# The first image's tokens are loaded and normalized among the turning of the weights

## Chip, cores and metric

The kernel runs on one core of a Trainium2 chip, as one program and one launch. The metric is the device time of that core in microseconds (us). A change of one part in five hundred, some 26 us, is about the smallest that a measurement of this kernel can tell from none.

A core has a matrix engine (TensorE, PE in the views), an engine for element-wise work and reductions (VectorE, DVE), one for functions of single elements (ScalarE, ACT), a general one (GpSimd, POOL), and a fifth that only issues transfers (SyncE, SP). Each takes its instructions in the order in which the program gives them. Transfers between the chip's memory (HBM) and the cores' memory (SBUF) are issued from the queues of SP, ACT and POOL. PE writes its results to a small memory divided into banks (PSUM).

## Reference

The input is `x`, four images of 64 x 64 tokens with 128 channels. Two layers follow each other; only the first part of the first layer bears on the change.

```python
# layer 0: group normalization, then a selective scan in three orders of the tokens
x = x + L0(_gn(x))
# layer 1: attention with 16 heads of 8 and a small network, then 64 experts of which tokens are picked
t = t + L1_attn(_ln_t(t)); t = t + L1_ffn(_ln_t(t))

def _gn(v, G=32, eps=1e-5):          # per image: mean and variance over 4 channels x 4096 tokens
    g = v.reshape(B_, H_, W_, G, C_ // G)
    m = jnp.mean(g, axis=(1, 2, 4), keepdims=True)
    s = jnp.var(g, axis=(1, 2, 4), keepdims=True)
    return ((g - m) / jnp.sqrt(s + eps)).reshape(v.shape)

xz = in_proj_w @ x                   # 128 channels to 2 x 256: x and z
u = silu(causal_conv1d(x, conv_w) + conv_b)              # 4 taps along the tokens
dt, B, C = split(x_proj_w @ u); delta = softplus(dt_w @ dt + dt_b)
h = h * exp(delta * A) + delta * u * B; y = sum(h * C)   # 16 states for each of 256 channels
y = (y + D * u) * silu(z)
```

The scan runs over the tokens forward, backward, and in an order that steps through 16 slices, each with weights of its own. `out_proj_w` brings the sum of the three back to 128 channels.

## The kernel before

The whole program is unrolled. Its work falls into stages.

**The weights.** `scan_weights` (L135) brings in `in_proj_w` and `out_proj_w` and turns them: PE transposes blocks of 128 x 128 into PSUM and DVE copies them out, to `w_z` and `w_out`. Then it does the same for each of the three orders ("directions"): `x_proj_w` (L155 to L163: 2 transposes, 12 small copies), `dt_proj_w` (L164 to L173: four transfers, two of them from SP's queue and two from ACT's), the biases and `D` (L174 to L180, seven transfers from ACT's queue with the taps) and the convolution, whose taps are folded into `in_proj_w`: for each of four taps DVE scales two blocks (L189), PE transposes them (L190) and DVE copies both out (L191). The raw weights lie in a pool `w_load`, closed at the end of the stage, with two slots of PSUM of its own.

**The inputs.** The class `Inputs` opens its pools after that (`i_const`, `i_big`, `i_piece`, `i_small`, and three slots of PSUM of two banks each), so that they may lie where the weights' pools lay. Its `norm(b)` (L270) brings in an image's tokens in four tiles `x_g` of 1024 tokens (512 KB each, L282, two slots), transposes each with eight transposes (L286), copies it to `xn` on ACT (L288), and takes statistics on DVE (L292). Two small matmuls sum them over groups of four channels (L297, L305), POOL raises the variance to the power -1/2 (L44, L45), and DVE scales the four pieces of `xn` (L313). `of_chunk` makes what the scan needs, for one direction and 1024 tokens: the convolution by PE (L378, 32 matmuls), silu on ACT (L385), the projection (L392, L395), `dt` (L414), softplus on ACT and PE (L418 to L436), the last addition on DVE (L441), and the product of delta and u (L446) for the first chunks. The results go to HBM from POOL's queue. The part from L414 to L441 is done for one chunk at a time (the flag `middle`), and each bank of PSUM that L436 fills comes free when L441 has read it. `gate` makes the silu of z.

**The scan of image 0.** `Scans.of_image` takes 384 steps of 128 rows (16 channels with 8 states) by 1024 tokens. A step is a scan on DVE (L538), the next step's product with B (L529) and the product with C (L543); ACT makes the exponentials (L522), PE sums over the states (L570). `decays` (L202), which comes first in this chain, waits until image 0 is normalized and then issues 96 small transfers of `A_log` from SP (L212).

**The order.** The code of the weights' stage is ordered by the framework's scheduler, which may also let an instruction of a later stage go ahead of it. Inside `tc.manual_schedule()` the program's own order holds on each engine. There, generators give their work in pieces that end with `yield`, and `Pace` runs them against each other. For all four images' inputs and the first image's scan it is this loop:

```python
            first = Pace(decays(nc, dirs, ws, inputs), scans.of_image(0, inputs.made, True))
            others = Pace(flow(inputs.pieces(range(nb)), 2, 10))
            while not first.done:
                others.run(1.5)
                first.run(1.0)
```

So `others` takes three pieces in every two rounds, one in a round and two in the next, and the scan one in each: the transfers and the exponential of a step in a round, its work on DVE in the next. `flow` keeps two of the inputs' generators going; the second starts when the one before has given ten pieces.

**The rest.** After that come image 0's opening, the attention of images 0 to 2 with the scans of images 1 to 3 beside it, image 3's attention, and the experts.

Of the kernel before, what the change touches and what calls it, by code (L numbers as in the profile page):

```python
# [11 lines left out]
F32 = mybir.dt.float32  # L12
# [4 lines left out]
P = 128  # L17
C = 128
L = 4096
NT = L // P  # L20
DI = 256
# [4 lines left out]
NC = L // T  # L26
NS2 = NS // 2
NB = DI // 8
# [103 lines left out]
        self.free += 1  # L132


def scan_weights(nc, const, load, load_ps, ident, in_proj_w, out_proj_w, dirs):  # L135

    w_z = const["fill"].tile([P, DI], F32, name="w_z")
    w_out = const["all"].tile([P, 2, C], F32, name="w_out")
    w_in = load.tile([P, 4, C], F32, tag="w_in", name="raw_in")
    nc.sync.dma_start(out=w_in, in_=in_proj_w.rearrange("(k p) c -> p k c", p=P))  # L140
    ps = load_ps.tile([P, 512], F32, tag="ps", name="ps_in")
    for m in range(2):
        nc.tensor.transpose(ps[:, m * P : (m + 1) * P], w_in[:, 2 + m, :], ident)
    nc.vector.tensor_copy(w_z, ps[:, :DI])
    raw = load.tile([P, DI], F32, tag="raw", name="raw_out")
    nc.sync.dma_start(out=raw, in_=out_proj_w)
    ps = load_ps.tile([P, 512], F32, tag="ps", name="ps_out")
    for m in range(2):
        nc.tensor.transpose(ps[:, m * P : (m + 1) * P], raw[:, m * P : (m + 1) * P], ident)
    nc.vector.tensor_copy(w_out.rearrange("p m c -> p (m c)"), ps[:, :DI])  # L150
    ws = []
    for i, d in enumerate(dirs):
        w = {}
        raw = load.tile([R + 2 * NS, DI], F32, tag="raw", name=f"raw_x{i}")
        nc.sync.dma_start(out=raw, in_=d["x_proj_w"])  # L155
        w["x"] = const["fill"].tile([P, 2, X_ROWS], F32, name=f"w_x{i}")
        nc.gpsimd.memset(w["x"], 0.0)
        for m in range(2):
            ps = load_ps.tile([P, 512], F32, tag="ps", name=f"ps_x{i}_{m}")
            k = R + 2 * NS  # L160
            nc.tensor.transpose(ps[:, :k], raw[:, m * P : (m + 1) * P], ident[:k, :k])
            for row, at, n in [(32 * g, 0, R) for g in range(4)] + [(B_ROW, R, NS), (C_ROW, R + NS, NS)]:
                nc.vector.tensor_copy(w["x"][:, m, row : row + n], ps[:, at : at + n])  # L163
        raw = load.tile([P, 2, X_ROWS], F32, tag="raw_dt", name=f"raw_dt{i}")  # L164
        nc.gpsimd.memset(raw, 0.0)
        for g in range(4):
            by = (nc.sync, nc.scalar)[g % 2]
            by.dma_start(out=raw[:, :, 32 * g : 32 * g + R], in_=d["dt_proj_w"].rearrange("(m p) r -> p m r", p=P))
        w["dt"] = const["fill"].tile([X_ROWS, 2, P], F32, name=f"w_dt{i}")
        ps = load_ps.tile([P, 512], F32, tag="ps", name=f"ps_dt{i}")  # L170
        for m in range(2):
            nc.tensor.transpose(ps[:X_ROWS, m * P : (m + 1) * P], raw[:, m, :], ident)
        nc.vector.tensor_copy(w["dt"].rearrange("r m p -> r (m p)"), ps[:X_ROWS, :DI])  # L173
        for name in ("conv_b", "dt_proj_b"):  # L174
            w[name] = const["fill"].tile([P, 2], F32, name=f"{name}{i}")
            nc.scalar.dma_start(out=w[name], in_=d[name].rearrange("(m p) -> p m", p=P))

        w["D"] = const["all"].tile([P, DI // 32], F32, name=f"D{i}")
        for g in range(4):
            nc.scalar.dma_start(out=w["D"][32 * g : 32 * g + 32], in_=d["D"].rearrange("(k p) -> p k", p=32))  # L180

        taps = load.tile([P, 2, 4], F32, tag="taps", name=f"taps{i}")
        nc.scalar.dma_start(out=taps, in_=d["conv_w"].rearrange("(m p) k -> p m k", p=P))
        w["conv"] = const["fill"].tile([P, 4, DI], F32, name=f"conv{i}")
        for k in range(4):
            ps = load_ps.tile([P, 512], F32, tag="ps", name=f"ps_cv{i}_{k}")
            for m in range(2):
                cut = load.tile([P, C], F32, tag="cut", name=f"cut{i}_{k}_{m}")
                nc.vector.tensor_scalar_mul(cut, w_in[:, m, :], taps[:, m, k : k + 1])  # L189
                nc.tensor.transpose(ps[:, m * P : (m + 1) * P], cut, ident)  # L190
            nc.vector.tensor_copy(w["conv"][:, k, :], ps[:, :DI])  # L191
        ws.append(w)
    for i, w in enumerate(ws):
        w["A"] = const["all"].tile([P, 2, NB // 2], F32, name=f"A{i}")
    return w_z, w_out, ws


def early(b, order, c):
# [17 lines left out]
class Inputs:  # L216
# [1 line left out]


    def __init__(self, tc, ctx, x, w_z, ws, cols, dram, ident):  # L220
        nc = self.nc = tc.nc
        self.x, self.w_z, self.ws, self.cols, self.dram, self.ident = x, w_z, ws, cols, dram, ident
        const = ctx.enter_context(tc.tile_pool(name="i_const", bufs=1))
        self.big = ctx.enter_context(tc.tile_pool(name="i_big", bufs=1))
        self.piece = ctx.enter_context(tc.tile_pool(name="i_piece", bufs=1))
        self.small = ctx.enter_context(tc.tile_pool(name="i_small", bufs=2))
        self.ps = ctx.enter_context(tc.tile_pool(name="i_ps", bufs=3, space=PSUM))

        group = const.tile([P, 32, 4], F32, name="group")
        nc.gpsimd.memset(group, 0.25)  # L230
        nc.gpsimd.affine_select(
            out=group, in_=group, compare_op=ALU.is_ge, fill=0.0,
            base=0, pattern=[[-4, 32], [0, 4]], channel_multiplier=1,
        )
        nc.gpsimd.affine_select(
            out=group, in_=group, compare_op=ALU.is_ge, fill=0.0,
            base=3, pattern=[[4, 32], [0, 4]], channel_multiplier=-1,
        )
        self.group = group.rearrange("p g r -> p (g r)")
        self.minus = const.tile([P, P], F32, name="minus")  # L240
        nc.vector.tensor_scalar_mul(self.minus, ident, -1.0)
        self.minus_one = column(nc, const, -1.0, "minus_one")
        self.made, self.sz, self.normed, self.sliced, self.gated = {}, {}, {}, {}, {}
        self.held, self.middle = 0, False

    def bank(self, name):
        while self.held == 3:
            yield WAIT
        self.held += 1
        return self.ps.tile([P, T], F32, tag="a", name=name)  # L250
# [4 lines left out]
    def pieces(self, images):  # L255

        for b in images:
            self.sz[b] = self.dram.tile([DI, L], F32, name=f"d_sz_{b}")
            yield self.norm(b)
            for order in range(3):  # L260
                if order == 2:
                    yield self.slices(b)
                for c in range(NC):
                    yield self.of_chunk(b, order, c)
                    third, at = divmod(order * NC + c, 3)
                    if at == 2:
                        yield self.gate(b, third)

    def norm(self, b):

        nc = self.nc
        while b - 1 in self.gated and self.gated[b - 1] < NC:
# [5 lines left out]
        nc.gpsimd.memset(xn[:, L + 3 :], 0.0)  # L278
        stats = self.small.tile([P, L // 512, 6], F32, tag="stats", name=f"stats_{b}")
        for g in range(NC):  # L280
            x_g = self.piece.tile([P, 8, C], F32, tag="x_g", bufs=2, name=f"x_{b}_{g}")
            nc.sync.dma_start(out=x_g, in_=xin[:, g * 8 : g * 8 + 8, :])  # L282
            yield
            ps = yield from self.bank(f"xt_{b}_{g}")
            for k in range(8):
                nc.tensor.transpose(ps[:, k * P : (k + 1) * P], x_g[:, k, :], self.ident)  # L286
            cut = xn[:, 3 + g * T : 3 + (g + 1) * T]
            nc.scalar.copy(cut, ps)  # L288
            self.leave()
            yield  # L290
            for k in range(2):
                nc.vector.bn_stats(stats[:, 2 * g + k, :], cut[:, k * 512 : (k + 1) * 512])  # L292
# [1111 lines left out]
def tile_kernel(tc, ctx, x, in_proj_w, dirs, out_proj_w, attn, gate, weight1, weight2, out):  # L1404


    nc = tc.nc
    nb = x.shape[0]
    ctx.enter_context(nc.allow_non_contiguous_dma(reason="small weight columns"))
    dram = ctx.enter_context(tc.tile_pool(name="dram", bufs=1, space=bass.MemoryType.DRAM))  # L1410
# [8 lines left out]
    scans = Scans(tc, scanning, ws, ident, None, dram)  # L1419
    with ExitStack() as fill:  # L1420
        consts = {"all": all_const, "fill": fill.enter_context(tc.tile_pool(name="w_fill", bufs=1))}
        with tc.tile_pool(name="w_load", bufs=2) as load, tc.tile_pool(
            name="w_load_ps", bufs=2, space=PSUM
        ) as load_ps:
            w_z, w_out, made = scan_weights(nc, consts, load, load_ps, ident, in_proj_w, out_proj_w, dirs)
        ws.extend(made)
        inputs = Inputs(tc, fill, x, w_z, ws, cols, dram, ident)
        scans.bank = Bank(fill.enter_context(tc.tile_pool(name="s_bank", bufs=2, space=PSUM)), 2)
        with tc.manual_schedule():
            first = Pace(decays(nc, dirs, ws, inputs), scans.of_image(0, inputs.made, True))  # L1430
# [118 lines left out]
```

## Time and profile before

| | |
|---|---|
| median of three runs | 12901.4 us (12900.43 to 12902.03) |
| the profiled execution, its own time | 12908.77 us |
| its span, first instruction to last | 12907.1 us |
| PE busy | 12125.7 us, 94% |
| ACT busy | 10718.9 us, 83% |
| DVE busy | 8730.9 us, 68% |
| POOL busy | 3129.4 us, 24% |
| first convolution of image 0 starts (L378) | 49.49 us |
| first scan starts (L538) | 126.04 us |

The profile is of one execution. Its times are microseconds from the start of its span, except for the mean of a group, which is in nanoseconds. A row of a timeline gives start and length, the engine ("ACTq" and "SPq" are transfers being issued from an engine's queue), the line, the tiles written and read, and in brackets how long the engine stood idle before and what ended that. In the chain of work that ended last each row is what the next one waited for. The three runs lie 7.4 us below the profiled execution in the middle.

### The profile page before, as it was taken

What the parts mean: (1) busy time and instruction counts of PE and PEld (TensorE: products, weight loads), DVE (VectorE), ACT (ScalarE), POOL (GpSimd) and SP (SyncE); (2) the same over time, 40 slices, a digit from 0 to 9 for tenths busy, and PEclk for the clock granted to TensorE, in tenths of its full rate; (3) what the DMA queues carried; (4) which work ended last, traced back from release to release, by engine and by line L of the source; (5) the groups of instructions that cost most, each with busy time, mean ns of one, the idle gap of its engine ahead of it and who ended that gap; (6) DMA issues with size and microseconds to landing.
All of it is one profiled execution on the core that took longest, in us unless ns stands there. A gap on an engine that the chain in (4) does not pass through costs nothing.

```text
span 12907.1 us, 215600 instructions
## 1 busy us (share of the span) xinstructions
PE 12125.7 (94%) x85447; PEld 3883.9 (30%) x85447; DVE 8730.9 (68%) x8912; ACT 10718.9 (83%) x10812; POOL 3129.4 (24%) x4007
## 2 busy tenths in 40 slices
PE   7888887599999999999999999999999999999996
PEld 3333333122222222333322222333222223333323
DVE  7999998788888877888887778888874211101112
ACT  5676766499999988999999889999998888888882
POOL 2324342232223222223232223232321000000000
PEclk9898988799999999999999999999999999999997
DMA  5666666555555455554554555545543100000004
GB/s 163 198 190 183 186 183 193 138 134 139 139 135 138 121 151 143 134 132 127 127 131 121 146 143 135 133 125 131 127 122 97 54 20 13 22 17 22 13 22 169
DMA packets 775661, 1553.29 MB, mean 120 GB/s; under 512 B 205198, under 2 KB 392134, under 8 KB 774390
## 3 DMA queue, kind: packets, MB, share of 16 engines
q1 hardware_dynamic: 590686, 1127.02, 33.7%
q0 software_dynamic: 142464, 302.77, 7.6%
q10 hardware_dynamic: 41496, 109.71, 3.3%
q8 instruction: 669, 10.96, 0.4%
q14 instruction: 346, 2.83, 0.1%
HBM read 1230.07 MB, written 308.81 MB: 119 GB/s over the span
## 4 chain that ended last, share of the span: by engine, by line
PE 80%; DVE 7%; ACT 5%; issue 4%; DMA 3%; SPq 1%; POOL 0%; ACTq 0%; DVEq 0%; POOLq 0%
PE s L917 36%; PE acc L931 29%; PE y L570 4%; PE cv L378 3%; DVE h L538 3%; PE sp L436 2%; PE fo L1069 1%; ACT e L922 1%; PE h L1059 1%; PE xd L392 1%; DVE dB L529 1%; DMA du<-d_du 1%; DMA w<-in_L_ffn_weight_dram 0%; DMA d_y<-o 0%; ACT e L424 0%
## 5 line engine op out<-in xcount | busy, mean ns | idle before, releaser
L922 ACT ACTIVATE e<-s 128x1024 f32<-128x1024 f32 x8192 | 7905.1, 1027 | 1107.0 <-PE s L917 940.4
L917 PE MATMUL s<-qm,qT 32*128 32x512 f32 x32768 | 5437.2, 642 | 112.5 <-DMA qT<-d_q 58.0
L931 PE MATMUL acc<-e,v 128*32 128x512 f32 x32768 | 4386.6, 607 | 24.4 <-ACT av L940 21.9
L917 PEld LDWEIGHTS s<-qm,qT 32*128 32x128 f32 x32768 | 1792.8, 183 | 3199.9 <-PE s L917 1408.6
L540 POOL COPY ends<-h 128x1 f32<-128x1 f32 x1152 | 1375.3, 1196 | 2875.1 <-DVE h L538 2866.0
L931 PEld LDWEIGHTS acc<-e,v 128*32 128x32 f32 x32768 | 646.9, 108 | 3162.8 <-issue 3021.4
L538 DVE TENSOR_TENSOR_SCAN h<-delta,ends,du 128x1024 f32<-128x1024 f32 x576 | 1351.6, 2347 | 196.6 <-ACT delta L522 162.2
L538 DVE TENSOR_TENSOR_SCAN h<-dA,ends,dB 128x1024 f32<-128x1024 f32 x576 | 1351.4, 2346 | 128.0 <-ACT dA L522 115.4
L529 DVE TENSOR_TENSOR dB<-du,B 128x1024 f32<-128x1024 f32 x768 | 929.6, 1210 | 657.1 <-PE y L570 595.0
L522 ACT ACTIVATE dA<-delta,A 128x1024 f32<-128x1024 f32 x768 | 888.0, 1156 | 147.3 <-DMA delta<-d_delta 146.3
L522 ACT ACTIVATE delta<-delta,A 128x1024 f32<-128x1024 f32 x768 | 887.1, 1155 | 137.6 <-PE y L570 127.8
L543 DVE TENSOR_TENSOR du<-h,C 128x1024 f32<-128x1024 f32 x768 | 936.5, 1219 | 0.1
L543 DVE TENSOR_TENSOR dB<-h,C 128x1024 f32<-128x1024 f32 x768 | 936.4, 1219 | 0.0
L529 DVE TENSOR_TENSOR du<-du,B 128x1024 f32<-128x1024 f32 x768 | 922.2, 1201 | 0.4 <-DMA B<-d_bc 0.3
L946 POOL DMA_DIRECT2D d_ctx<-av x512 | 259.9, 517 | 1248.2 <-ACT av L940 1242.7
L378 PE MATMUL cv<-xn,conv 128*128 128x512 f32 x1024 | 490.5, 632 | 33.0 <-DVE xn L313 17.3
L570 PE MATMUL y<-du,sel 128*32 128x256 f32 x6144 | 483.9, 387 | 17.3 <-DVE du L543 17.3
L570 PE MATMUL y<-dB,sel 128*32 128x256 f32 x6144 | 486.8, 389 | 4.3 <-DVE dB L543 3.4
L538 DVE TENSOR_TENSOR_SCAN h<-delta,du 128x1024 f32<-128x1024 f32 x192 | 438.7, 2285 | 45.8 <-ACT delta L522 37.8
L599 POOL DMA_DIRECT2D d_y<-o x512 | 328.5, 671 | 562.9 <-DVE o L586 430.8
L538 DVE TENSOR_TENSOR_SCAN h<-dA,dB 128x1024 f32<-128x1024 f32 x192 | 438.6, 2284 | 36.8 <-ACT dA L522 35.9
L564 POOL DMA_DIRECT2D d_du<-x_delta x272 | 154.4, 568 | 1132.2 <-DVE x_delta L563 1069.1
(255 smaller groups left out, 7643.6 us busy)
## 6 DMA issues: line engine op xcount, KB each, us to landing
delta<-d_delta SPq DMA_DIRECT2D x768, 512.0 KB
du<-d_du SPq DMA_DIRECT2D x576, 512.0 KB
du<-d_du ACTq DMA_DIRECT2D x192, 512.0 KB
d_u<-u POOLq DMA_DIRECT2D x48, 1024.0 KB, 5.7
B<-d_bc SPq DMA_DIRECT2D x96, 512.0 KB
C<-d_bc SPq DMA_DIRECT2D x96, 512.0 KB
d_delta<-r POOLq DMA_DIRECT2D x48, 1024.0 KB, 5.7
us<-d_u SPq DMA_DIRECT2D x384, 128.0 KB
```

Of the source, the lines that this page charges most:

```text
L378: nc.tensor.matmul(ps[:, cut], w["conv"][:, k, m * P : (m + 1) * P], reads(k, g), start=(k == 0), stop=(k == 3))
L522: nc.scalar.activation(tiles["delta", s], t, AF.Exp, scale=A)
L529: nc.vector.tensor_mul(tiles["du", s], du, spread[order, c, "B", j % 2])
L538: nc.vector.tensor_tensor_scan(h, dA, dB, first, ALU.mult, ALU.add)
L540: nc.gpsimd.tensor_copy(ends[order, c][:, at : at + 1], h[:, T - 1 :])
L543: nc.vector.tensor_mul(dB, h, spread[order, c, "C", j % 2])
L570: nc.tensor.matmul(y[32 * g : 32 * g + 32, : T // 4], self.sel[:, j // 2, :], hC[:, 256 * g : 256 * g + 256], start=(j == 0), stop=(j == 3),)
L599: nc.gpsimd.dma_start(out=to.rearrange("p (i j) -> p i j", i=SLICES)[:, :, at : at + n], in_=rows.rearrange("p (i j) -> p i j", i=SLICES),)
L917: nc.tensor.matmul(s_ps[:, k, :], qT[at : at + 32, kc * P : (kc + 1) * P], queries[j, qb][at : at + 32, :], start=True, stop=True,)
L922: nc.scalar.activation(e, s_ps, AF.Exp, scale=1.0 / math.sqrt(D))
L931: nc.tensor.matmul(accs[j, qb][32 * k : 32 * k + 32, :], v[:, kc, h * VW : h * VW + 32], es[i][k // 2][:, k % 2, :], start=(kc == 0), stop ...
L946: nc.gpsimd.dma_start(out=self.context[b][h * D : h * D + D, cut], in_=av[32 * k : 32 * k + D, :])
```

## The change

`norm` of image 0 leaves the loop above and is done in the weights' stage. For that `Inputs` is made before the weights, with its own slots of PSUM beside the weights' two; its pool `i_piece` is opened after the stage, by `open`. `norm` is given the pool that its tiles `x_g` come from: for image 0 that is `w_load` with four slots, so that each of the four loads has a tile of its own; for the others it is `i_piece` with two, as before. `scan_weights` becomes a generator with a pause after `w_z` and `w_out` and after each direction; it appends to the list `ws` itself. The whole stage now stands in `tc.manual_schedule()`, in this order: `w_z` and `w_out`; the four loads of `x`, their transposes and copies, and the statistics of the first three; direction 0; the last statistics and the first small matmul; direction 1; the second small matmul; direction 2; the power and the scaling.

No computation is added or removed, and no transfer.

```diff
-def scan_weights(nc, const, load, load_ps, ident, in_proj_w, out_proj_w, dirs):
-    w_z = const["fill"].tile([P, DI], F32, name="w_z")
-    w_out = const["all"].tile([P, 2, C], F32, name="w_out")
+def scan_weights(nc, const, load, load_ps, ident, in_proj_w, out_proj_w, dirs, w_z, w_out, ws):
...
     nc.vector.tensor_copy(w_out.rearrange("p m c -> p (m c)"), ps[:, :DI])
-    ws = []
+    yield
     for i, d in enumerate(dirs):
...
+        w["A"] = const["all"].tile([P, 2, NB // 2], F32, name=f"A{i}")
         ws.append(w)
-    for i, w in enumerate(ws):
-        w["A"] = const["all"].tile([P, 2, NB // 2], F32, name=f"A{i}")
-    return w_z, w_out, ws
+        yield
...
-        self.piece = ctx.enter_context(tc.tile_pool(name="i_piece", bufs=1))
...
+    def open(self, ctx):
+        self.piece = ctx.enter_context(self.tc.tile_pool(name="i_piece", bufs=1))
...
-            yield self.norm(b)
+            if b not in self.normed:
+                yield self.norm(b, self.piece, 2)
...
-    def norm(self, b):
+    def norm(self, b, pool, bufs):
...
-            x_g = self.piece.tile([P, 8, C], F32, tag="x_g", bufs=2, name=f"x_{b}_{g}")
+            x_g = pool.tile([P, 8, C], F32, tag="x_g", bufs=bufs, name=f"x_{b}_{g}")
...
+        w_z = consts["fill"].tile([P, DI], F32, name="w_z")
+        w_out = all_const.tile([P, 2, C], F32, name="w_out")
+        inputs = Inputs(tc, fill, x, w_z, ws, cols, dram, ident)
         with tc.tile_pool(name="w_load", bufs=2) as load, tc.tile_pool(
             name="w_load_ps", bufs=2, space=PSUM
-        ) as load_ps:
-            w_z, w_out, made = scan_weights(nc, consts, load, load_ps, ident, in_proj_w, out_proj_w, dirs)
-        ws.extend(made)
-        inputs = Inputs(tc, fill, x, w_z, ws, cols, dram, ident)
+        ) as load_ps, tc.manual_schedule():
+            weights = scan_weights(
+                nc, consts, load, load_ps, ident, in_proj_w, out_proj_w, dirs, w_z, w_out, ws
+            )
+            norm = inputs.norm(0, load, NC)
+            next(weights)
+            for _ in range(2 * NC):
+                next(norm)
+            for _ in range(2):
+                next(weights)
+                next(norm)
+            for _ in chain(weights, norm):
+                pass
+        inputs.open(fill)
```

More of the change, by code (lines that the diff above doesn't have):

```diff
@@ L220, in __init__ @@
     def __init__(self, tc, ctx, x, w_z, ws, cols, dram, ident):
-        nc = self.nc = tc.nc
+        self.tc, nc = tc, tc.nc
+        self.nc = nc
         self.x, self.w_z, self.ws, self.cols, self.dram, self.ident = x, w_z, ws, cols, dram, ident
```

## The prediction

> **What bounds the kernel now.** I read the page first, then the chain of work that ended last, cut to the first 160 us, then the timeline of ACT and PE there, then the stretches between the landmarks, and last the waits of DVE and PE while image 0 is scanned. The engines over the stages (columns: stretch, length, busy time of each engine with its count, clock, share of the DMA engines, GB/s):
>
> ```profile
> 0.00:49.50 49.50, 21.60 (x77) 13.96 (x77) 23.44 (x100) 6.62 (x6) 4.13 (x19) 0.92 0.32 56
> 49.50:124.70 75.20, 62.43 (x142) 25.48 (x143) 7.30 (x9) 30.24 (x27) 5.13 (x8) 0.91 0.46 117
> 124.70:2185.00 2060.30, 1763.11 (x6599) 707.23 (x6597) 1925.28 (x1400) 1495.06 (x1194) 729.11 (x798) 0.90 0.66 188
> ...
> 2430.00:12907.10 10477.10, 10234.23 (x78404) 3104.77 (x78404) 6597.66 (x7057) 9160.99 (x9563) 2341.92 (x3113) 0.98 0.41 106
> ```
>
> From 2430 us on PE bounds (98% busy). Between 125 and 2185 us DVE does (93%). Before 49.5 us nothing is busy: a chain of short steps and transfers. All stages follow each other, so a microsecond less before 49.49 is a microsecond less at the end, unless a later stage gives it back. The chain there:
>
> ```profile
> 5.92 4.67 DMA dt_proj_b<-_L_conv_dt_proj_b_b_dram
> 11.09 2.36 DMA raw_dt<-in_L_conv_dt_proj_w_dram
> ...
> 32.01 0.44 DVE conv L191
> 32.49 1.98 PE xt L286 x8
> 34.49 4.07 DMA x<-in_x_dram
> ```
>
> Small transfers until 13.5 us, then the turning of the weights until 32.43, then the tokens, of which tiles 2 and 3 are only asked for at 34.49, when the slots come free. From 32.43 to the first convolution (49.49) it is 17.06 us. Two more places matter, both from ACT's timeline:
>
> ```profile
> 4.90 0.46 ACTq L183 DMA_DIRECT2D taps<-in_L_conv_conv_w_dram  x1
> ...
> 32.51 1.28 ACT L288 ACT_TABLE_LOAD   x1 [32.51 <-DVE conv L191]
> ...
> 625.75 1.01 ACT L395 COPY xds<-xd 104x1024 f32<-104x1024 f32 x1 [2.91 <-PE xd L392]
> 625.76 0.52 ACTq L508 DMA_DIRECT2D du<-d_du  x1
> ```
>
> The first: ACT issues small transfers from the start, since the copies of x come behind them. The second: a transfer behind a copy that waits for PE goes out in the instant that the copy starts. So a waiting copy holds the transfers behind it in ACT's queue.
>
> **What the skill says.** PSUM — Partial Sum Buffer, "Engine vs sequencer instructions": the queues of ScalarE, VectorE and GpSimdE are strictly first in, first out; the rows at 625.75 agree. DMA: Bandwidth & Descriptors, "Issuing engines are not separate DMA queues": all transfers share 16 engines, so a second queue saves only issuing time; issuing is 0.4 to 0.5 us here, and that is what ACT will have too much of. The same page, "Anatomy of one DMA", gives about 2 us fixed per transfer; here the small `raw_dt` took 2.36 us from issue to use. TensorE: Matmul & The Clock Gate, "What's actually happening": half clock after an idle window of about 3.4 us; the trace agrees, the convolution that starts at 49.49 runs at 0.50 until about 55.6.
>
> **The change part by part.** Removed: the stretch of 17.06 us behind the weights, except its tail. Moved: 4 loads (2 MB) on SP ahead of the `raw_x` and `raw_dt` loads, 32 transposes, 4 ACT copies, 8 statistics. Nothing is added but the waits that an order written out brings. Step by step, as the new program order puts it:
>
> 1. Loads. SP issues `raw_in`, `raw_out` and the four tiles by about 3.8 us. `raw_out` was used at 4.80; the pair issued at 34.49 was used at 38.60 and by 40.56, so 2.0 us a tile: the last lands at 4.8 + 4 x 2.0 = 12.8. (At the 191 GB/s of the page's row for 4 to 8 us it is 15.7.) Eight transposes, 1.98, and their wait: the fourth copy starts at 15.0. Copies and statistics before it are hidden in the loading.
> 2. ACT's queue. The transfers of direction 0 stand behind the fourth copy: 2 `raw_dt` 0.94, 2 biases 0.9, 4 `D` 1.9, taps 0.4, so 4.15: the taps are issued at 19.1 instead of 4.9, and land 2.4 later, 21.5. `raw_x` on SP has come by then, behind the tiles; the transposes and copies of `w_x` and `w_dt` are done by 19.5.
> 3. Direction 0. A tap is 1.19 us (DVE's rows at 27.61, 28.80 and 29.98), four 4.75: 26.3. Queued behind on DVE: the last statistics and the sum, 1.29 + 0.37, 28.0; matmul 0.6, 28.6.
> 4. Direction 1. Transposes 0.5, 12 copies 1.05, `w_dt` 0.4, taps 4.75: 6.7, at 35.3. Its transfers are issued by 23.3, landed by 26. Four small DVE steps 0.75, matmul 0.6: 36.6.
> 5. Direction 2: 6.7, at 43.3. Its taps wait for a slot until 26, and land by 33.
> 6. Tail: copy 0.2, POOL 0.85 (L44, L45), first scaling 0.82, hand-overs 0.3: the convolution starts at 45.4. Before 49.49: 4.1 less.
>
> The bounds: tiles at 191 GB/s cost 2.9 of it; if ACT's queue did not hold, the taps would not wait and some 7 us more come off. The half clock at the start of the convolution I count as before; if PE stayed warm, half of 6.1, 3.0, is gained, else at most 0.4 lost. SP's 96 small `A` transfers (40 us) now start near 30 instead of 36.15 and are needed at 115.6: nothing, there is 40 us of cover.
>
> 7. The loop after. `norm` took 13 pieces of `others` before the first chunk; without them the scan starts nine rounds earlier, at round 20 for 29. Nine is odd, so the rounds in which `others` gets one piece and two change places. The order on PE, ACT and SP stays the same; on DVE 13 of the 48 pairs of L441 fall behind the scan step (2.35 + 1.2 + 1.2 less overlap, 4.65 us) that they stood before, and some statistics of images 1 to 3. POOL's small copies and stores shift with them, needed much later.
>
> ```profile
> DVE r L441 <- PE sp L436: 8.3, 9, 2.1
> DVE gms L307 <- PE gv L305: 3.1, 3, 1.6
> ...
> PE dt L414 <- DVE r L441: 16.3, 13, 2.5
> ```
>
> The first two rows (waits of DVE: total, times, longest) can shrink: 5.5 of the 8.3 are at the displaced pairs, and L307 is displaced three times. The third shows the price: the next chunk's second half of L414 needs the bank that L441 empties. It is held 4.65 longer; ACT works meanwhile on the first half (2 us), and PE came late itself. By the starts of L441, L414 and L418 in the trace twelve pairs put the next chunk back by 0.1 to 4.1 us, 22.6 together; the pair after each stood ready for 0 to 9.8 us, and what exceeds that is 2.6 us. So between -6 (8.6 gained, 2.6 lost) and +23 (none absorbed). I take 0: the chain in that stage changes between DVE and the chunks' PE and ACT steps all the time, and gain and loss are both of the size of what the trace can tell.
>
> Sum: -4.1. Against the profiled execution, 12908.8 - 4.1 = 12904.7; the runs stand 7.4 lower: 12897.3, so 12897.
>
> **The rivals.** *ACT's queue does not hold.* Then the taps are there early and direction 0 begins at 15: 11 us less, 12890. For it: ACT's small issues ran freely before 17 us. Against: 625.75, and several like it.
>
> *Nothing arrives.* The first scan waits for `du` (on the chain, 113.43 to 124.62), and transfers may fall otherwise: 12901. Against: `du` itself is made by a chain from the convolution without a gap.
>
> *Slower: the displaced L441.* Place: the 12 pairs with a next chunk behind them, in the scan of image 0. If the lost 4.65 us are passed on whole, 12 x 4.65 = 56, less 4: 12953; with the 22.6 counted, 12920. It decides against the forecast from (26 + 4) / 12 = 2.5 us a pair. For it: the chain of that stage runs through PE's steps (L378 and L436 together a third of it between 700 and 1900 us), and L414 directly follows L441 at most pairs. Against: the counted mean is 1.9 before any slack, and DVE, which does the same work, idles only 6%.
>
> *The order is not what is written.* If the scheduler still moved the loads, the start would be as before; the loop's shift would remain.
>
> **How the numbers follow.** A change below 0.2%, 26 us, can hardly be told from none. Forecast (-10 to +4 around the start and the loop: 12888 to 12905) 0.72. ACT free 0.08, at 12890. Nothing arrives 0.07, at 12901. Slower loop 0.13, from 12910 to 12953, a little over half of it above 12927. So same 0.90, slower 0.08, faster 0.02: no mechanism here is worth 26 us. The range, 12885 to 12920, leaves the upper part of the slow case and the rare ones out.
>
> **What would show it.** Loads of x at 2 to 4 us on SP, all four; ACT's first `raw_dt` issue at the start of the fourth copy, near 15; first tap (L189) near 21.5; L378 near 45.4; first L538 near 122. In the loop, DVE waits at L441 and L307 shrunk, those at L529 and L538 (43.9 and 60.1 us now) unchanged within 10. The forecast is wrong if the taps come before 17 or after 26, or if the stretch from the first scan to the last L441 (126 to 2185) is over 15 us longer or shorter.

## The result, and the profile after

The median of the changed kernel is 12,934.5 us (12 runs, 12,920.0 to 12,943.4), that of the kernel before beside it 12,906.2 us (12 runs, 12,900.4 to 12,918.4). The ratio is 1.0021, with a 95% interval of 1.0013 to 1.0029: the change costs 17 to 37 us. The forecast was 12,897. The interval is some 10 us wide to either side, so with 12 runs of each kernel less than the 26 us named ahead can be told from none. The two profiled executions differ by 21.6 us of span (12,928.7 for 12,907.1), which lies between 17 and 37; the working below is made against that pair. Lines of the loop have moved by one (L441 is now L442, L538 is L539, L414 is L415), those of the weights by two back (L189 is L187).

The stages first (columns as in the prediction's first fence: stretch, length, busy time of PE, PEld, DVE, ACT and POOL, clock, DMA share, GB/s). The second line runs from the first L530 to the end of the last L442, as the line 124.70 to 2185.00 did before.

```profile
0.00:50.13 50.13, 19.46 (x76) 12.57 (x77) 22.88 (x100) 6.62 (x6) 3.98 (x19) 0.65 0.41 56
...
126.30:2206.20 2079.90, 1777.63 (x6606) 710.07 (x6604) 1931.21 (x1404) 1495.51 (x1194) 671.02 (x799) 0.91 0.66 187
```

The convolution starts at 50.13, not at 45.4 as forecast, and not at 49.49 as before. The stretch of image 0's scan is 2079.90 us for 2060.30, with the same work on ACT (1495.5) and 0.3% more on DVE, and with 14.5 us more of PE. Followed at the starts of scan step L539 against L538, the difference is +1.6 us at the first step, +9.1 at the step that was at 933, +16.4 at the last one of image 0 (2194), +20.2 at 2470 and +21.6 at the end. So nearly all of the loss is made between 126 and 2470 us, 14.8 us of it between the first and the last scan step of image 0.

The chain of work at the start of the changed kernel (start, length, what):

```profile
5.26 7.18 DMA x<-in_x_dram
...
17.81 2.79 DMA D<-in_L_conv_D_dram
...
22.84 0.68 PE ps_cv L188 x2
```

Loading of x and small transfers take up the first 20 us, as forecast, and then the taps follow with a wait for PE in each. ACT's timeline shows the queue that the prediction feared:

```profile
13.68 1.01 ACT L289 COPY xn<-xt 128x1024 f32<-128x1024 f32 x1 [0.22 <-PE xt L287]
14.59 1.11 ACTq L166 DMA_DIRECT2D raw_dt<-in_L_conv_dt_proj_w_dram  x2
...
19.87 0.47 ACTq L181 DMA_DIRECT2D taps<-in_L_conv_conv_w_dram  x1
```

The fourth copy starts at 13.68, the first `raw_dt` of direction 0 is issued behind it at 14.59, the taps at 19.87 (forecast 15.0 and 19.1).

Now the scan of image 0. DVE's waits between 126 and 2290 us (total, times, longest):

```profile
DVE h L539 <- ACT dA L523: 40.1, 29, 4.8
DVE dB L530 <- DMA du<-d_du: 34.5, 9, 14.3
DVE h L539 <- ACT delta L523: 29.7, 20, 4.6
...
DVE r L442 <- PE sp L437: 1.7, 4, 0.9
```

The same three waits in the kernel before:

```profile
DVE h L538 <- ACT dA L522: 38.3, 23, 4.8
DVE h L538 <- ACT delta L522: 21.8, 15, 4.6
DVE dB L529 <- DMA du<-d_du: 16.1, 4, 12.8
```

A pair is the two additions L441 (now L442) of one chunk. The wait there has nearly gone (8.3 to 1.7 us), as forecast. But the wait for loads of `du` has grown from 16.1 to 34.5 us, those for ACT's exponentials from 60.1 to 69.8. (The longest wait for `du`, 12.8 and now 14.3 us, falls behind image 0's scan; within it these waits grew from 3.3 to 20.2.) Who is behind it shows in the answer on PE's products `dt` (idle time of PE's weight loads and of its matmuls, added, that the pair ended, times; then how long ACT waited for the products). Changed kernel, L415:

```profile
  DVE r L442: 125.4, 40
...
  ACT e L419: 70.8, 48
```

Kernel before, L414:

```profile
  DVE r L441: 36.8, 23
...
  ACT e L418: 32.9, 38
```

A close look at one displaced pair shows how the lateness travels. The kernel before, PE and then ACT, just after the pair L441 of chunk 4 ran from 276.66 on DVE:

```profile
277.93 1.13 PE L414 MATMUL dt<-xds,w_dt 8*128 8x512 f32 x4 [0.77 <-DVE r L441]
279.06 1.99 PE L336 MATMUL z<-xn,w_z 128*128 128x512 f32 x4
```

```profile
279.22 1.11 ACT L418 ACTIVATE e<-dt,dt_proj_b 128x1024 f32<-128x1024 f32 x1
...
280.37 0.52 ACTq L508 DMA_DIRECT2D du<-d_du  x1
```

The changed kernel, where one scan step stands ahead of that pair, which ran at 282.66:

```profile
283.93 2.07 PE L415 MATMUL dt<-xds,w_dt 8*128 8x512 f32 x4 [5.64 <-DVE r L442]
285.94 3.78 PE L337 MATMUL z<-xn,w_z 128*128 128x512 f32 x4
```

```profile
286.05 1.11 ACT L419 ACTIVATE e<-dt,dt_proj_b 128x1024 f32<-128x1024 f32 x1 [5.59 <-PE dt L415]
...
287.20 0.52 ACTq L509 DMA_DIRECT2D du<-d_du  x1
```

PE stands 5.64 us at the second half of `dt`, until the first addition of the pair is through. There are three slots of PSUM: the pair's sums have two, the first half of `dt` the third, and the second half gets the slot that the pair's first addition empties. (ACT has read the first half by 280.46, but its slot is not used for the second.) When PE goes on, `dt` takes 2.07 us for 1.13, and the four products behind it 3.78 for 1.99: the granted clock from 283.9 to 289.7 is 0.50. So it is half clock after the idle time, as the Trainium skill has it (TensorE: Matmul & The Clock Gate, "What's actually happening": an idle window of about 3.4 us). ACT waits 5.59 us for that half, and the load of `du` that stands behind it in ACT's queue is issued at 287.20 for 280.37. Of these 6.8 us the changed kernel had 1.1 already at the load of `du` before (273.53 for 272.40), so 5.7 are due to the late pair. The lateness of one pair thus reaches three things that feed the scan, none of which is the next pair: PE's products, ACT's exponentials and the loads of `du`. Whether it costs anything depends on what DVE waits for just then. This pair cost nothing (+1.6 us at the first scan step, +1.5 at 300 us). From just before one late pair to just before the next, the difference to the kernel before changes by -2.9 to +3.5 us, and 12.6 of the 14.8 us come from chunk 16 on.

### The profile page after: what moved, and what is told of

Same layout as the page of the kernel before. It is cut to its first block, busy times and chain, and to the rows that moved or that the text cites. A ratio compares the mean times of both kernels' runs of the same rounds, so it can differ in the third digit from the quotient of the medians.

```text
span 12928.7 us, 215589 instructions
## 1 busy us (share of the span) xinstructions
PE 12136.4 (94%) x85447; PEld 3884.2 (30%) x85447; DVE 8730.8 (68%) x8912; ACT 10720.2 (83%) x10812; POOL 3047.3 (24%) x4007
## 4 chain that ended last, share of the span: by engine, by line
PE 79%; DVE 7%; ACT 5%; issue 4%; DMA 3%; SPq 1%; POOL 0%; ACTq 0%; DVEq 0%; POOLq 0%
PE s L918 35%; PE acc L932 29%; PE y L571 4%; PE cv L379 3%; DVE h L539 3%; PE sp L437 2%; PE fo L1070 1%; ACT e L923 1%; PE h L1060 1%; PE xd L393 1%; DVE dB L530 1%; DMA du<-d_du 1%; ACT ln L430 1%; ACT e L425 0%; ACT s L427 0%
## 5 line engine op out<-in xcount | busy, mean ns | idle before, releaser
L932 PE MATMUL acc<-e,v 128*32 128x512 f32 x32768 | 4388.1, 607 | 23.9 <-ACT av L941 21.5
L541 POOL COPY ends<-h 128x1 f32<-128x1 f32 x1152 | 1300.0, 1129 | 3008.8 <-DVE h L539 2987.9
L539 DVE TENSOR_TENSOR_SCAN h<-delta,ends,du 128x1024 f32<-128x1024 f32 x576 | 1350.6, 2345 | 206.3 <-ACT delta L523 170.2
L539 DVE TENSOR_TENSOR_SCAN h<-dA,ends,dB 128x1024 f32<-128x1024 f32 x576 | 1350.3, 2344 | 130.4 <-ACT dA L523 117.3
L530 DVE TENSOR_TENSOR dB<-du,B 128x1024 f32<-128x1024 f32 x768 | 928.6, 1209 | 665.0 <-PE y L571 600.2
L530 DVE TENSOR_TENSOR du<-du,B 128x1024 f32<-128x1024 f32 x768 | 920.9, 1199 | 0.1
L539 DVE TENSOR_TENSOR_SCAN h<-delta,du 128x1024 f32<-128x1024 f32 x192 | 438.5, 2284 | 47.8 <-ACT delta L523 38.3
L539 DVE TENSOR_TENSOR_SCAN h<-dA,dB 128x1024 f32<-128x1024 f32 x192 | 438.3, 2283 | 36.5 <-ACT dA L523 33.3
```

What stands on the lines that cost most here:

```text
L530: nc.vector.tensor_mul(tiles["du", s], du, spread[order, c, "B", j % 2])
L539: nc.vector.tensor_tensor_scan(h, dA, dB, first, ALU.mult, ALU.add)
L541: nc.gpsimd.tensor_copy(ends[order, c][:, at : at + 1], h[:, T - 1 :])
L932: nc.tensor.matmul(accs[j, qb][32 * k : 32 * k + 32, :], v[:, kc, h * VW : h * VW + 32], es[i][k // 2][:, k % 2, :], start=(kc == 0), stop ...
```

## The experiments

**Is it the exchanged rounds or the start?** `Pace` adds the share of a round to a credit and gives a piece for each whole unit of it. Two kernels set the credit with which `others` begins, so that rounds with one and with two pieces change places and nothing else does.

```
after_turned_back: the changed kernel        before_turned: the kernel before
 others = Pace(flow(...))                     others = Pace(flow(...))
+others.credit = 0.5                         +others.credit = 1.0
```

> The changed kernel with the credit of `others` begun at 0.5, so that rounds with one and with two pieces stand as in the kernel before, and the prologue of the change is kept. Theory (the exchanged rounds cost the time, the prologue costs 0.6 us): the median comes back to within 6 us of the kernel before, some 12,907, ratio 1.0000 to 1.0004. Rival (the prologue or the tiles of its own cost the time, whatever the rounds): it stays at the changed kernel's time, +20 to +28 us, ratio near 1.002.

> The kernel before with the credit of `others` begun at 1.0: the prologue is untouched and only the rounds with one and with two pieces are exchanged, as in the changed kernel. Theory (exchanged rounds): +16 to +27 us, ratio 1.0013 to 1.0021, with the loss spread from 400 us to the end and lying in DVE's waits at the scans L538 and the multiplications L529. Rival (prologue or tiles): 0, within 4 us.

Measured: `after_turned_back` 12,911.7 us for 12,908.2 of the kernel before, and the ratio, which is not that of these two medians, is 1.0000 (0.9992 to 1.0009). `before_turned` 12,933.3 us, ratio 1.0019 (1.0012 to 1.0026), with +19.6 us between the first and the last scan step of image 0. Each direction of the swap moves the whole loss: the rounds make it, and the new start, with the tiles of its own, costs nothing that these runs can tell.

**Which of the things that the rounds move?** The swap displaces 13 pairs and also statistics of the norms. In `before_pairs` only the 13 pairs, with what follows them, are put behind the scan step of their round; on DVE they then stand where `before_turned` has them, and the statistics where the kernel before has them.

```
-for m in range(2):
-    nc.vector.tensor_add(r[:, m, :], r[:, m, :], banks[m])
-    self.leave()
-keep("delta", r)
...
+def last():
+    for m in range(2):
+        nc.vector.tensor_add(r[:, m, :], r[:, m, :], banks[m])
+        self.leave()
+    keep("delta", r)
...
+if (b * 3 + order) * NC + c in BEHIND:     # the 13 chunks
+    self.behind.append(last)
+else:
+    last()
...
 first.run(1.0)
+while inputs.behind:
+    inputs.behind.pop()()
```

> The kernel before, with the pair of additions L441 (and the multiplication and store behind it) of the thirteen chunks 4, 6, 10, 16, 18, 22, 28, 30, 34, 40, 42, 46 and 47 put behind the scan step of its round, and all else, the statistics of the norms too, where it was. Theory (late pairs cost the time): +12 to +22 us, most of what the exchanged rounds cost. Rival (displaced statistics L292 and L307, or TensorE's and ScalarE's pieces, cost it): 0 to +6 us.

Measured: 12,933.1 us, ratio 1.0020 (1.0013 to 1.0027), +21.9 us between the first and the last scan step. That is the whole loss of `before_turned`, even a little more: displaced statistics add nothing. PE (until the pair L444) and ACT (for `dt`) wait as in the changed kernel:

```profile
  DVE r L444: 120.9, 40
...
  ACT e L420: 66.9, 47
```

**What of the late pair costs?** A pair does two things: it empties two slots of PSUM, and it makes `delta` and `du`, which are stored and loaded again. `before_stores` leaves the additions where they were in all 13 chunks and defers only the rest.

```
 for m in range(2):
     nc.vector.tensor_add(r[:, m, :], r[:, m, :], banks[m])
     self.leave()
+def last():
     keep("delta", r)
...
```

> The kernel before. In the same thirteen chunks as in the experiment with the late pairs, the two additions L441 stay where they were, so that they empty their PSUM banks on time; what follows them (the store of delta, the multiplication L446 and the store of du) comes behind the scan step. Theory (a late pair costs because it holds the banks, and PE's next L414 waits for them): -3 to +6 us, PE's waits for L441 at L414 stay near 16 us. Rival (it costs because delta and du are stored late and loaded late): +14 to +25 us, as with the late pairs, with DVE's waits for the loads of du at L529 near 35 us.

Measured: 12,909.3 us for 12,910.7 of the kernel before, ratio 0.9998 (0.9990 to 1.0007); -0.3 us between the first and the last scan step. PE's idle time before `dt` until the pair is that of the kernel before:

```profile
  DVE r L443: 35.5, 21
```

So the late stores cost nothing, and what costs is that the additions themselves come late. The stores of `delta` went out 2.7 to 9.9 us later in 11 of the 13 chunks (4.4 to 9.9 in `before_pairs`, and there in all 13), and those of `du` in the three chunks of image 0 6.7 us later (9.0 to 9.1), so they were late, though less than with the late pairs. The other ten of the 13 chunks belong to images 1 to 3, whose `delta` the scan of image 0 doesn't load, and most of the loss is made beside these. That a late addition costs by holding its slot is read from PE's waits at `dt` (120.9 us in `before_pairs`, 35.5 here); no run here frees the slot in another way while the additions stay late.

`after_half` was meant for that: the changed kernel with its 13 late pairs, but with the first addition of every pair one piece earlier, so that one slot is free sooner.

```
-yield
-for m in range(2):
-    nc.vector.tensor_add(r[:, m, :], r[:, m, :], banks[m])
-    self.leave()
+nc.vector.tensor_add(r[:, 0, :], r[:, 0, :], banks[0])
+self.leave()
+yield
+nc.vector.tensor_add(r[:, 1, :], r[:, 1, :], banks[1])
+self.leave()
```

> The changed kernel, credit at 0 as it is, so the thirteen pairs stay late; but the first addition of every pair is written one piece ahead of the second, so that one of the two banks comes free before the scan step again. Theory (the late pair costs because the next chunk's second half of L414 needs one bank): most of the loss goes, within 8 us of the kernel before (12,903 to 12,916), and PE's waits for L442 at L415 fall below 20 us. Rival (both banks, or the late end of the pair, count): 12,925 to 12,935 as the changed kernel.

Measured: 12,912.0 us for 12,909.0, ratio 1.0002 (0.9994 to 1.0010); -4.2 us between the first and the last scan step, where the changed kernel has +14.8. PE's idle time before `dt` until the first addition (L440):

```profile
  DVE r L440: 21.6, 13
```

Weight loads and matmuls together stand 21.6 us, for 125.4 in the changed kernel; the matmuls alone, which the expectation meant, 12.4 for 55.1. But the kernel is not the one that was meant. The program goes on with a chunk that needs a slot only when one has been given back, so an addition that is written earlier draws later pieces forward, and ACT's work follows in another order too. In the trace the second additions of only two of the 13 pairs (chunks 4 and 6) still stand a scan step later than in the kernel before; from chunk 10 on no pair is late. For chunk 30, as an example, the second addition stands behind the 244th scan step as in the kernel before, where the changed kernel has it behind the 245th. The run thus agrees with the others (no late pairs and no loss), but whether one early slot would be enough beside late pairs is not shown. Which of the three late things costs how much is not shown either: here DVE waits 30.6 us for loads of `du` and is as quick as before, with less waiting for the exponentials (52.7).

**A third order of the rounds.** With a credit of 0.5 in the kernel before, DVE keeps all its pairs and statistics where they were, and pieces of the other engines come one earlier.

```
 others = Pace(flow(...))
+others.credit = 0.5
```

> The kernel before with the credit of `others` begun at 0.5: on DVE the pairs of L441 keep the places of the kernel before, but pieces of the other engines stand differently against the scan steps. If only DVE's places of the pairs cost time: within 4 us of before. If what counts is where a piece's TensorE and ScalarE work stands: a difference of over 8 us, either way (5 in 10 each way); the direction is open.

Measured: 12,942.9 us, ratio 1.0025 (1.0015 to 1.0035), +27.8 us in the scan of image 0. It is the slowest of the three orders though no pair is displaced, and DVE's largest wait, 43.9 us and 17 times before, is now

```profile
DVE dB L529 <- PE y L570: 71.6, 28, 6.0
```

PE's products for the chunks stand ahead of the products `y` (L570) that empty `dB`. That is read from the waits; no run here isolates it. PE's idle time before `dt` until the pair is longer here too, 67.7 us for 36.8. So late pairs are one way to lose time in this stage and not the only one. The kernel before has the best of the three orders.

**Why was the start not 4 us earlier?** Three kernels, all with the rounds turned back (credit at 0.5), so that the start alone differs. The first draws the next tap's cuts (the two blocks that DVE scales by a tap) ahead of the copy of this one.

```
-for k in range(4):
-    for m in range(2): ... cut ... transpose
-    nc.vector.tensor_copy(w["conv"][:, k, :], ps[:, :DI])
+now = list(cuts(0))
+for k in range(4):
+    for m in range(2): ... transpose of now[m]
+    now = list(cuts(k + 1)) if k < 3 else None
+    nc.vector.tensor_copy(w["conv"][:, k, :], ps[:, :DI])
```

> The changed kernel with the credit at 0.5, and the cuts of the next tap written ahead of the copy of this one (four cut tiles). Theory (the written order makes a tap 1.46 us, the scheduler of before had drawn cuts ahead): a tap 1.1 to 1.2 us, the convolution some 3.2 us earlier, at 46.5 to 47.5 for 50.1. Rival (a tap is bound by DVE's own work or PE): the tap stays above 1.4 us, the convolution at 50.

> The kernel with the credit at 0.5 and the cuts ahead, once more, beside the two others: some 6 us (first scan) below the kernel before, 12,895 to 12,905 where that has 12,908.

DVE's rows for a tap show it. Changed kernel, kernel before, and `after_taps`:

```profile
22.41 0.48 DVE L187 TENSOR_SCALAR cut<-raw_in,taps 128x128 f32<-128x128 f32 x2 [3.67 <-DMA raw_dt<-_L_conv_dt_proj_w_b_dram]
23.54 0.42 DVE L189 COPY conv<-ps_cv 128x256 f32<-128x256 f32 x1 [0.65 <-PE ps_cv L188]
23.88 0.47 DVE L187 TENSOR_SCALAR cut<-raw_in,taps 128x128 f32<-128x128 f32 x2
```

```profile
27.61 0.47 DVE L189 TENSOR_SCALAR cut<-raw_in,taps 128x128 f32<-128x128 f32 x2
28.45 0.42 DVE L191 COPY conv<-ps_cv 128x256 f32<-128x256 f32 x1 [0.37 <-PE ps_cv L190]
28.80 0.47 DVE L189 TENSOR_SCALAR cut<-raw_in,taps 128x128 f32<-128x128 f32 x2
```

```profile
23.52 0.42 DVE L195 COPY conv<-ps_cv 128x256 f32<-128x256 f32 x1 [0.26 <-PE ps_cv L193]
23.86 0.47 DVE L186 TENSOR_SCALAR cut<-raw_in,taps 128x128 f32<-128x128 f32 x2
24.25 0.42 DVE L195 COPY conv<-ps_cv 128x256 f32<-128x256 f32 x1
```

From copy to copy it is 1.46 us in the changed kernel: both cuts, then 0.65 us of wait for the transposes, then the copy. In the kernel before it is 1.19, where the row of two cuts is the second half of one tap and the first of the next: the scheduler had drawn a cut ahead. With both cuts ahead it is 0.73, less than expected, since DVE doesn't wait at all in the middle rounds. The convolution starts at 43.52, 6.9 us earlier than in `after_turned_back` (50.38), and the first scan step 6.0 us earlier than in the kernel before; at the end of image 0's scan 5.6 of it are still there (4.9 and 3.3 in the repeat). The medians: 12,900.1 for 12,910.7 (0.9993, 0.9984 to 1.0002), and once more 12,904.8 for 12,909.0 (0.9998, 0.9989 to 1.0006). Both intervals hold 1: that it beats the kernel before is likely from the first scan step, but the times do not show it.

The second kernel takes ACT's `raw_dt` and taps of all directions ahead of the copies of x.

```
+for i, d in enumerate(dirs):
+    ask(i, d)        # raw_dt halves on ACT, taps; three tiles each
+yield
 for i, d in enumerate(dirs):
     ...
```

> The changed kernel with the credit at 0.5, and ACT's transfers of raw_dt and taps of all three directions written ahead of the copies of x (three tiles each). Theory (the waiting copies hold the taps of direction 0): its first cut at 16.5 to 18 us for 22.4, the convolution 4 to 6 us earlier, at 44 to 46. Rival (something else is late there, the loads on SP or the completion of transfers): first cut after 20, the convolution within 2 us of 50.

The theory fell: the first cut comes at 24.00, the convolution at 51.69. The median is 12,912.0 us for 12,910.7, ratio 0.9999 (0.9990 to 1.0008). ACT's timeline:

```profile
9.43 0.37 ACTq L159 DMA_DIRECT2D taps<-in_L_conv_conv_w_dram  x1
13.10 0.96 ACTq L155 DMA_DIRECT2D raw_dt<-_L_conv_dt_proj_w_b_dram  x2
...
17.61 2.84 ACT L302 COPY xn<-xt 128x1024 f32<-128x1024 f32 x3
```

ACT's own issues now stand still, first until 9.43 and then until 13.10, and the copies of x behind them start at 17.61 for 9.05. The taps are early (issued at 9.43 for 19.87), but DVE's first cut stands behind the statistics of these copies. The profile names no work of an engine that ended there; the DMA engines were 87% busy or more, with x, from 4 until 12 us. What held these issues is not settled; that small transfers come through slowly beside 2 MB of loads would fit it. The waiting copies were thus not the only thing in the way.

The third has both edits, and direction 0's weights turned ahead of the tokens.

```
 next(weights)
+next(weights)
 for _ in range(2 * NC):
     next(norm)
-for _ in range(2):
-    next(weights)
-    next(norm)
+next(norm)
+next(weights)
+next(norm)
```

> Both of these edits together, and direction 0's weights turned ahead of the tokens' transposes and copies instead of behind them. Worked out: transfers of direction 0 landed near 6, its weights turned by 13, tokens transposed and copied by 18.5, statistics by 20, direction 1 by 26.5, direction 2 by 33, convolution at 35 to 37 us for 49.5 in the kernel before. Time 8 to 14 us below the kernel before, near 12,897, ratio 0.9989 to 0.9994, if the scan stage passes it on; if the scan stage's steps give it back, a ratio of 1.000 with the convolution early all the same.

The convolution in PE's timeline:

```profile
40.13 16.09 PE L398 MATMUL cv<-xn,conv 128*128 128x512 f32 x32 [2.46 <-DVE xn L333]
```

The convolution starts at 40.13, 9.4 us earlier than before, the first scan step 9.2, the last of image 0 10.9. The median is 12,904.3 for 12,910.7, ratio 0.9996 (0.9988 to 1.0004), and the profiled span only 1.0 us shorter: of the 10.9 us, 5.1 were lost between the last scan step and 2470 us and 4.8 after it.

**Both together.** `after_taps` with the first addition a piece earlier, the two diffs above added.

> The kernel with the credit at 0.5 and the cuts ahead, and the first addition of each pair a piece earlier as well. If earlier banks help where no pair is late too: 3 to 12 us below the same kernel without it (12,888 to 12,897 where that has 12,900). If DVE only waits for PE's L436 products instead: the same or up to 10 us slower, with waits at the first addition.

12,907.1 us for 12,909.0, ratio 0.9996 (0.9987 to 1.0004), and beside 12,904.8 of the same kernel without it: nothing gained. As in `after_half`, the additions come up to two scan steps earlier and the pieces move with them, so this is no test of the earlier slot alone.

## Why the prediction was wrong, step by step

*Steps 1 and 2 (loads, ACT's queue)* were near: the fourth copy starts at 13.68 (15.0 forecast), the taps are issued at 19.87 (19.1), the first tap starts at 22.41 (21.5). ACT's transfers did come behind the copies, so the rival with a queue that doesn't hold fell. `after_queue` agrees that their place in the queue held the taps, and shows that the 7 us named for a queue that doesn't hold are not to be had by an exchange: the transfers then hold the copies.

*Steps 3 to 5 (the directions)* failed in size. A tap was taken as 1.19 us, from rows of a kernel whose order the scheduler had chosen. In the order as written it is 1.46, and twelve of them make 3.2 us; directions 1 and 2 took 8.1 us each for 6.7. Direction 0 ended at 28.3 (26.3), direction 1 at 38.7 (35.3), direction 2 at 48.1 (43.3). Of these last 4.8 us, 3.2 are the taps, 0.9 the later first tap, and the rest is spread over small steps. With that the gain of 4.1 us at the convolution became a loss of 0.6. `after_taps` shows the term: with the cuts drawn ahead the start is early, even by more than forecast.

*Step 6 (tail)* held: 2.0 us from the last copy to the convolution, for 2.1. The aside on the `A` transfers did not: SP issued the first at 10.98 us, not near 30, and 32 of them before 28.4, among the stage's own. In so far the order of SP's queue was not the written one; the loads of x stood where they were written.

*Step 7 (the loop)* is what decided. Its count of 13 pairs, each one scan step later, was exact. Its price was not, in two terms. The delay of the twelve next chunks was put at 22.6 us; in the traces the second half of their `dt` starts 2.9 to 4.9 us later each (against the first half, changed kernel against the kernel before), 47.5 together, and ACT's L419 on it 38.8. And the delay was set against the time that the pair after each stood ready, which left 2.6 us. That is the step that failed most: a late chunk does not first show at the next pair. It shows at the scan steps between: loads of `du` issued late behind ACT's waiting L419, exponentials late on ACT, PE at half clock after standing. These have less slack than the next pair, and the loss in image 0's scan was 14.8 us (changed kernel), 19.6 (`before_turned`) and 21.9 (`before_pairs`), so as a mean 1.2 to 1.8 us for each of twelve pairs. That the counted 1.9 lies so near is luck: the delay was nearly twice as long, and DVE passed on about half of it, unevenly, nothing at the first late pairs. The upper bound of that step, +23, was right; taking 0 inside it was not.

*The rival "the displaced L441"* was the one that came true, in place and mechanism, with the luck in its size just named. It was sized to 12,920 with the 22.6 counted, less a gain of 4.1 at the start that did not come; with that gone, and 0.6 lost, it reads 12,925, and the kernel before stood 4.8 us higher in these runs (12,906.2 for 12,901.4), which makes it 12,929 for 12,934.5. In the profiled pair 2.5 us came on top in waits for `du` and `y` between 2200 and 2275, and 2.7 later. The point from which it decides, 2.5 us a pair, was set with the start's gain in it. The chance of 0.13 was too low: PE's wait of 16.3 us at L414 was on the page, and the argument against it rested on DVE's idle share of 6% and on its slack at one line.

*The sign that the prediction named* worked: the stretch from the first scan step to the last pair was to stay within 15 us, and it went from 2056.8 to 2076.1 us, 19.3 more (the last pair is itself one of the 13). The waits named beside it did not tell: those at L529 and L538 stayed within 10 us (43.9 to 43.1, 60.1 to 69.8), because the list left out the loads of `du`, whose waits grew by 18.4.

## What to carry to other kernels

When a round of one stream takes pieces of another at a rate that is no whole number, removing an odd number of rounds ahead of it shifts the whole pattern; look at what the shift does to instructions that free a scarce buffer, and not only at those that produce data. Where the program gives out work by what has been freed, an edit that frees earlier moves other work too: compare the orders in the traces before such a run is read. Slack is to be measured at every wait of the bounding engine, not at the next instance of the delayed instruction; and transfers that stand in a waiting engine's queue count among the delayed things. A step's duration from a kernel that a scheduler arranged is not valid for the same step in a written order: where DVE and PE hand each other small tiles, write the next producer ahead of the copy.

## What was not expected of the hardware

Two profiled executions of one kernel (`after_taps`) had spans of 12,890.9 and 12,904.0 us, of which 5.9 had come about by the step at 2470 and 7.2 after it. A gain of 5 us at the start can therefore be read at the first scan step, and hardly at the end.

PE's stand of 5.64 us for a slot of PSUM cost more than itself: the four products `dt` behind it took 0.94 us longer and four products `z` 1.79 longer. Over image 0's scan PE was busy 14.5 us more for nearly the same number of matmuls (6606 for 6599).
